# Decoder of four layers: the last cross-attention's maxima, with two steps over the short last piece of keys joined into one

## Chip, core and metric

The kernel runs on one core of a Trainium2 chip. The metric is the device time of one execution in microseconds (us), the median of several runs. Engine names are those of the profile: PE is TensorE's matmul (PEld its weight loads), DVE VectorE, ACT ScalarE, POOL GpSimd, SP SyncE.

## The reference, cut to what matters

The reference is a decoder of four layers, each an attention, a cross-attention with a context of 6404 rows, and a feed-forward part. The change touches the last layer's cross-attention alone. With x of 1024 rows, width 128, 16 heads of 8, the reference does

```
q = split_heads(x @ Wq.T + bq)            # 16 x 1024 x 8
k = split_heads(ctx @ Wk.T + bk)          # 16 x 6404 x 8
v = split_heads(ctx @ Wv.T + bv)
scores = q @ k.T / sqrt(8)                # masked keys: -1e9
ctx = softmax(scores) @ v
out = ctx @ Wo.T + bo
```

For the softmax, each row's largest score is taken off before the exponential. The kernel works out these maxima first ("maxima"), and the scores, exponentials and products with the values after that ("core").

## The kernel before

**Tiles and stages.** Heads go in four groups g of four, and queries in two halves h of 512. A pair of group and half is called a unit here, n = 2g + h, n = 0 to 7. `l3_xattn` (L1783) first has a part that makes keys, queries and values and the maxima of unit 0 with nothing beside them (its `m2` tiles, which hold the maxima's scores in PSUM, have three buffers, L1798). Then a loop over n = 0 to 6 (L1826) runs `pairs_core` for unit n with the maxima of unit n + 1 as its `beside`; here `m2` has two buffers, `s` three and `acc` one (L1819). Unit 7 runs in a stage of its own with nothing beside it.

**Core.** `pairs_core` (L1327) goes over the keys in tiles of 128. 6404 keys make 51 tiles, and the last holds 4 keys. For each tile, and each of two pairs of heads, it makes the scores `s` (keys by 512 queries, one matmul for each of the pair's two heads), and ScalarE takes the exponential into `p` (L1375). Products with the values go into `acc` one tile later (`late`, L1346). After the last tile the values of tiles 49 and 50 follow, then `acc` is copied to `oT` (`copy`, L267: in turn by VectorE, L271, and ScalarE, L273), and `pairs_norm` (L1391) transposes `oT` into an `m2` tile (L1396), takes reciprocals of the sums (L1399) and writes `o` (L1401).

**Maxima.** `pairs_max` (L1281) is a generator. It goes over the keys in pieces of 512, `c` = 0 to 12, of which the last has 260 keys, and over four blocks of 128 queries: 52 steps. A step is called for pair 0 and pair 1; each call takes an `m2` tile, makes two matmuls into it (one for each head) and a reduction by VectorE (L1303) over its 2 x 512 or 2 x 260 elements. After the last step the generator runs `pairs_neg` (L1308): a last reduction `r` (L1313), six casts and two subtractions that split the negated maximum into three parts in `mpad` (L1316 to L1319), and for each pair four transposes of `mpad` into one `m2` tile (L1323) and an addition onto the queries `qP` (L1325). The next unit's scores need these.

**The order around the change.** Scores, maxima and values of these units are held in the order in which they are written (L265). At the head of each tile, `pairs_core` takes a step by `next(beside, None)` (L1354), and calls it for both pairs between the scores of pair 0 and those of pair 1. What the generator has left after the last tile is run behind the last values (L1386). There are 52 steps and 51 tiles, so one step and `pairs_neg` come there. The prologue, the part ahead of unit 0, calls each step by itself. `l0_attn` uses `pairs_max` too, with `causal` set.

Of the kernel before, what the change touches and what calls it, by code (L numbers as in the profile page):

```python
# [25 lines left out]
BANK = 512  # L26
# [185 lines left out]
class Decoder:  # L212
# [1068 lines left out]
    def pairs_max(self, ps, pool, qP, kP, h, mpad, nk=NK, causal=None):  # L1281

        nc = self.nc
        chunks = h + 1 if causal is not None else (nk + BANK - 1) // BANK
        mx = pool.tile([P, 4, 4, chunks], F32, tag="mx", name="mx")
        for c in range(chunks):
            for t in range(4):  # L1290
                q0 = h * BANK + t * P
                a, b = c * BANK, min((c + 1) * BANK, nk if causal is None else q0 + P)

                def step(pair, a=a, b=b, q0=q0, t=t, c=c):
                    diag = causal is not None and b == q0 + P
                    m = ps.tile([P, 2, BANK], F32, tag="m2", name="m2")
                    for j in range(2):
                        r = slice(64 * j, 64 * j + 64)
                        self.matmul(m[:, j, :b - a], lhsT=qP[pair][r, q0:q0 + P], rhs=kP[pair][r, a:b], start=True, stop=not diag)
                    if diag:  # L1300
                        for j in range(2):
                            self.matmul(m[:, j, b - a - P:b - a], lhsT=causal[:, 1, :], rhs=causal[:, 0, :], start=False, stop=True)
                    nc.vector.tensor_reduce(mx[:, t, 2 * pair:2 * pair + 2, c:c + 1], m[:, :, :b - a], AX.X, ALU.max)  # L1303

                yield step
        self.pairs_neg(ps, pool, qP, h, mpad, mx)

    def pairs_neg(self, ps, pool, qP, h, mpad, mx):  # L1308
# [625 lines left out]
```

## Time and profile before

| | us |
|---|---|
| median of 3 runs | 6131.01 (6130.72 to 6139.10) |
| the profiled execution | 6133.59 |
| its span | 6131.8 |
| PE busy | 5705.8 (93%) |
| DVE busy | 3756.3 (61%) |
| ACT busy | 3097.7 (51%) |
| POOL busy | 2254.4 (37%) |
| prologue's maxima, about | 4820 to 4941 |
| units 0 to 6, about | 4941 to 5843 |
| unit 7, about | 5843 to 5940 |

Times inside the span are counted from its start. A line of a timeline gives the start, the length, the engine, the line of the kernel, the operation with the tiles written and read, and how many instructions were merged; in brackets stands how long the engine had been idle and what released it. In a table of stretches the granted clock is TensorE's: 1.00 is full speed. Line numbers are those of the kernel before; those behind L1303 move by 9 or less in the changed one (L1323 becomes L1332).

### The profile page before, as it was taken

How to read it: one execution, taken by the hardware profiler on the slowest of the kernel's cores; microseconds unless marked ns; L12 is line 12 of the kernel's file. 1: busy time of each engine (PE TensorE's matmuls, PEld its weight loads, DVE VectorE, ACT ScalarE, POOL GpSimd, SP SyncE). 2: the span in 40 equal slices, each digit the busy share in tenths (PEclk: the TensorE clock that was granted, in tenths of full speed). 3: DMA queues.
4: the chain of work that ended last, by engine and by line, in shares of the span. 5: the costliest groups of instructions: out<-in, count | busy, mean ns of one | idle time of the engine just before them, and what ended most of it. 6: DMA issues, size and time to landing. Idle time of an engine off the chain costs nothing. (4 is left out here: it accounts for less than half of the span.)

```text
span 6131.8 us, 72192 instructions
## 1 busy us (share of the span) xinstructions
PE 5705.8 (93%) x29144; PEld 2049.1 (33%) x29144; DVE 3756.3 (61%) x4571; ACT 3097.7 (51%) x4041; POOL 2254.4 (37%) x1088
## 2 busy tenths in 40 slices
PE   5899999999999999999899968999989689999999
PEld 2333333333333433333375433111124211111126
DVE  6587777777777777776235461100025799999923
ACT  2434444444444444444321326899941167888872
POOL 2057767676776767678341530100001000000000
PEclk7899999999999999999999978999989689999989
DMA  3000000000000000000000013200022100000000
GB/s 114 4 1 1 1 1 1 1 1 1 1 1 1 1 1 1 1 17 18 30 9 11 1 66 92 77 17 1 1 93 71 54 1 22 1 22 1 1 6 30
DMA packets 65199, 117.97 MB, mean 19 GB/s; under 512 B 10474, under 2 KB 46672, under 8 KB 63200
## 3 DMA queue, kind: packets, MB, share of 16 engines
q1 hardware_dynamic: 64288, 110.08, 5.6%
q8 instruction: 228, 3.74, 0.2%
q10 hardware_dynamic: 576, 3.28, 0.1%
q14 instruction: 107, 0.88, 0.0%
HBM read 81.88 MB, written 31.42 MB: 18 GB/s over the span
## 5 line engine op out<-in xcount | busy, mean ns | idle before, releaser
L741 POOL TENSOR_TENSOR tot<-tot,p 128x1024 f32<-128x1024 f32 (+1 forms) x800 | 1889.6, 2362 | 584.7 <-ACT p L732 569.2
L732 ACT ACTIVATE p<-p,drop,keep 128x1024 f32<-128x1024 f32 (+1 forms) x816 | 1011.8, 1240 | 1321.8 <-DVE p L731 1260.1
L669 DVE TENSOR_REDUCE mx<-m 128x2 f32<-128x1024 f32 (+1 forms) x832 | 982.1, 1184 | 496.5 <-PE m L668 480.0
L1303 DVE TENSOR_REDUCE mx<-m 128x2 f32<-128x1024 f32 (+4 forms) x928 | 1027.0, 1156 | 92.8 <-PE m L265 82.4
L731 DVE TENSOR_TENSOR p<-s,every 128x1024 f32<-128x1024 f32 (+1 forms) x816 | 991.2, 1215 | 73.2 <-PE s L726 34.6
L1375 ACT ACTIVATE p<-s 128x512 f32<-128x512 f32 (+4 forms) x1620 | 819.5, 589 | 239.1 <-PE s L265 238.3
L668 PE MATMUL m<-kT,qT 64*128 64x512 f32 (+1 forms) x3328 | 888.6, 606 | 12.3 <-DVE mx L669 11.6
L1372 ACT ACTIVATE p<-s 128x1024 f32<-128x1024 f32 x918 | 843.9, 1187 | 31.6 <-PE s L1367 24.1
L726 PE MATMUL s<-qT,kT 64*128 64x512 f32 (+1 forms) x3264 | 837.6, 596 | 16.6 <-DVE p L731 15.4
L713 PE MATMUL acc<-p,v 128*64 128x512 f32 (+1 forms) x3264 | 809.4, 606 | 4.8 <-ACT p L732 4.1
L1346 PE MATMUL acc<-p,v 128*8 128x512 f32 (+2 forms) x3672 | 621.9, 597 | 0.0
L265 PE MATMUL m<-kP,qP 64*128 64x512 bf16 (+4 forms) x1856 | 371.5, 396 | 101.8 <-DVE mx L1303 56.9
L726 PEld LDWEIGHTS s<-qT,kT 64*128 64x128 f32 (+1 forms) x3264 | 321.7, 185 | 412.5 <-issue 342.1
L668 PEld LDWEIGHTS m<-kT,qT 64*128 64x128 f32 x3328 | 280.7, 185 | 504.1 <-DVE mx L669 371.6
L265 PE MATMUL acc<-p,v 128*9 128x512 f32 (+2 forms) x3240 | 422.2, 594 | 0.0
L265 PE MATMUL s<-qP,kP 64*128 64x512 bf16 (+4 forms) x1620 | 384.0, 387 | 8.9 <-ACT p L1375 6.1
L713 PEld LDWEIGHTS acc<-p,v 128*64 128x64 f32 (+1 forms) x3264 | 198.8, 136 | 550.8 <-issue 456.1
L1367 PE MATMUL s<-qP,kP 48*128 48x512 bf16 (+2 forms) x1836 | 281.0, 384 | 2.7 <-ACT p L1372 1.9
L271 DVE COPY oT<-acc 128x512 f32<-128x512 f32 x14 | 9.7, 689 | 404.5 <-PE acc L1346 395.7
L387 POOL MEMSET mpad<- 128x512 f32 x2 | 1.1, 530 | 637.0 <-PE m L1456 600.4
L265 PEld LDWEIGHTS <-qP 64*128 64x128 bf16 x1856 | 122.8, 96 | 318.8 <-issue 261.9
L265 PEld LDWEIGHTS <-kP 64*128 64x128 bf16 (+1 forms) x1620 | 83.6, 94 | 352.4 <-issue 347.5
(484 smaller groups left out, 4446.7 us busy)
## 6 DMA issues: line engine op xcount, KB each, us to landing
kd<-part SPq DMA_DIRECT2D x156, 128.0 KB, 1.8
wb<-expert_weights SPq DMA_DIRECT2D x30, 512.0 KB, 3.6
kP<-kd SPq DMA_DIRECT2D x24, 512.0 KB, 3.6
kP<-kd SPq DMA_DIRECT2D x48, 192.0 KB, 4.5
w_expert<-in_Y_w SPq DMA_DIRECT2D x8, 768.0 KB, 4.2
qd<-part SPq DMA_DIRECT2D x36, 128.0 KB, 1.8
qP<-qd SPq DMA_DIRECT2D x16, 256.0 KB, 5.3
ctxT<-in_ctxT ACTq DMA_DIRECT2D x4, 800.5 KB, 6.3
```

Source lines behind the costliest of these rows:

```text
L265: return self.tc.keep_in_program_order(self.nc.tensor.matmul(*a, **k))
L668: nc.tensor.matmul(m[:, j, :b - a], lhsT=qT[r, q0:q0 + P], rhs=kT[r, a:b], start=True, stop=True)
L669: tc.keep_in_program_order(nc.vector.tensor_reduce(mx[:, t, :, c:c + 1], m[:, :, :b - a], AX.X, ALU.max))
L713: nc.tensor.matmul(acc[64 * j:64 * j + 64, :], lhsT=v[:n, t, 64 * j:64 * j + 64], rhs=pr[:n, j, :], start=t == 0, stop=t == NKT - 1, tile_ ...
L726: nc.tensor.matmul(s[:n, j, :], lhsT=kT[r, t * P:t * P + n], rhs=qT[r, hs], start=True, stop=True)
L731: tc.keep_in_program_order(nc.vector.tensor_tensor(pr[:n], s[:n], every[:n], ALU.add))
L732: nc.scalar.activation(pr[:n], pr[:n], AF.Exp, bias=drop[:n, t:t + 1], scale=keep[:n, t:t + 1])
L741: nc.gpsimd.tensor_tensor(tot[:n], tot[:n], pr[:n], ALU.add)
L1303: nc.vector.tensor_reduce(mx[:, t, 2 * pair:2 * pair + 2, c:c + 1], m[:, :, :b - a], AX.X, ALU.max)
L1346: matmul(acc[32 * j:32 * j + v.shape[3], off:], lhsT=v[:n, t, 4 * g + j, :], rhs=ws[j][:n, :BANK - off], start=t == 0, stop=t == nkt - 1, ...
L1372: nc.scalar.activation(p2[:n], both[:n], func)
L1375: nc.scalar.activation(pp[j][:n, :w], ss[j][:n, :w], func)
```

## The change

Steps whose piece has at most 320 keys (BANK * 5 // 8) are not given out at once when `causal` is not set: two are kept and given out as one function that calls both. With 6404 keys these are the four steps of the last piece, so the generator gives 48 + 2 = 50 steps. A joined step calls pair 0 of both steps, then pair 1 of both. The 51st call of `next` then finds no step, and runs what stands behind the loop, `pairs_neg`.

```
+        short = []
         for c in range(chunks):
             for t in range(4):
...
-                yield step
+                if causal is None and b - a <= BANK * 5 // 8:
+
+                    short.append(step)
+                    if len(short) == 2:
+                        one, other = short
+                        short = []
+                        yield lambda pair, one=one, other=other: (one(pair), other(pair))
+                else:
+                    yield step
         self.pairs_neg(ps, pool, qP, h, mpad, mx)
```

## The prediction

> **What bounds the kernel now.** Seen whole, TensorE is busy 93% of the span and VectorE 61%, but that says little about this stage, so I went from the page to the timelines of the last cross-attention. A *unit* is one group of heads by one half of the queries (51 tiles); beside units n = 0 to 6 the maxima of unit n+1 are worked out. On the page, the maxima's reductions are one of the costliest groups:
>
> ```profile
> L1303 DVE TENSOR_REDUCE mx<-m 128x2 f32<-128x1024 f32 (+4 forms) x928 | 1027.0, 1156 | 92.8 <-PE m L265 82.4
> ```
>
> Inside a unit VectorE is the bound: 98 reductions over full pieces run back to back in 114.03 us (timeline of VectorE, from 5200.98), 1.164 us each, so 2.33 us a tile of two; a tile lasts 2.35. What can be won or lost lies at the ends of units. Busy time by stretch, first a unit's inside, then an end (columns: length, busy us and count of TensorE, its weight loads, VectorE, ScalarE, GpSimd, then granted clock and DMA):
>
> ```profile
> 5072.00:5184.00 112.00, 106.57 (x760) 20.75 (x755) 112.00 (x97) 98.53 (x192) 0.00 (x0) 1.00 0.07 21
> 5184.00:5201.00 17.00, 12.52 (x86) 4.26 (x80) 10.71 (x25) 7.14 (x15) 0.00 (x0) 0.81 0.19 65
> ```
>
> TensorE's timeline over the end of unit 0 (start, length, line, tile, count, wait):
>
> ```profile
> 5056.53 0.39 PE L265 MATMUL s<-qP,kP 64*128 64x512 bf16 x2
> 5056.76 0.28 PE L265 MATMUL m<-kP,qP 64*128 64x260 bf16 x2
> 5057.24 0.29 PE L265 MATMUL m<-kP,qP 64*128 64x260 bf16 x2 [0.20 <-DVE mx L1303]
> ...
> 5061.24 0.38 PE L265 MATMUL s<-qP,kP 64*4 64x512 bf16 x2
> ...
> 5062.59 2.15 PE L265 MATMUL acc<-p,v 128*9 128x512 f32 x16
> 5064.67 0.40 PE L265 MATMUL m<-kP,qP 64*128 64x260 bf16 x4
> 5068.68 1.09 PE L1323 MATMUL m<-ident,mpad 128*128 128x128 f32 x4 [3.61 <-DVE mpad L1317]
> 5069.55 1.06 PE L1396 MATMUL m<-ident,oT 128*128 128x128 f32 x4
> 5070.54 1.11 PE L1323 MATMUL m<-ident,mpad 128*128 128x128 f32 x4
> 5071.59 0.43 PE L265 MATMUL s<-qP,kP 64*128 64x512 bf16 x2
> ```
>
> Tile 48 starts at 5056.53, tile 49 at 5058.89, tile 50 (4 keys) at 5061.24. The left-over 52nd step is at 5064.67. Then TensorE waits 3.61 us for the chain of pairs_neg, and the next unit starts at 5071.59. While TensorE waits, the copy of `acc` (0.58 us on ScalarE, from 5064.77) is hidden.
>
> **The change, part by part.** Both programs' orders, compared engine by engine, differ on TensorE and VectorE alone, and only at the ends of units and of the part ahead of them. No instruction goes or comes: VectorE still does eight reductions of 520 elements a unit.
>
> *The doubled steps.* Tiles 48 and 49 now each hold four score pairs and four reductions between `s` of pair 0 and `s` of pair 1, and `m2` has two buffers. The third `m` waits for the first reduction, the fourth for the second, and TensorE, which issues these in order, holds `s` of pair 1 and the values behind them. From the timelines: a reduction of 520 elements starts 0.33 us after its matmul (5061.55 to 5061.88), lasts 0.69, and the next follows after 0.62; its buffer's matmul comes 0.09 after its end. Tile 48 (a run of two full and two short reductions stands in the trace from 5054.83 to 5058.40): the first short one runs 5057.09 to 5057.78, the second ends at 5058.40, the fourth `m` goes at 5058.49, `s` of pair 1 at 5058.60, the values 0.21 later take 0.97 (5060.26 to 5061.24), so tile 49 starts at 5059.78: **+0.89**. Tile 49 in the same way: products at 5060.00, first reduction at 5060.33, fourth product at 5061.73, values done at 5063.02, against 5061.24: **+0.89** again. VectorE does not hide this: 4 x 0.62 = 2.5 us would fit a tile, the ring of two does not.
>
> *The chain moved ahead of tile 50.* The 51st `next()` runs pairs_neg, and its eight transposes stand before tile 50's scores. The last reduction ends at 5062.88. From the part ahead of the units, where nothing else is between, VectorE's and TensorE's rows give the rest:
>
> ```profile
> 4935.14 0.37 DVE L1313 TENSOR_REDUCE r<-mx 128x16 f32<-128x208 f32 x1
> ...
> 4938.19 0.69 DVE L1325 TENSOR_TENSOR qP<-qP,m 128x512 bf16<-128x512 bf16 x1 [1.27 <-PE m L1323]
> ```
>
> ```profile
> 4937.07 1.09 PE L1323 MATMUL m<-ident,mpad 128*128 128x128 f32 x4 [3.33 <-DVE mpad L1317]
> 4938.94 1.11 PE L1323 MATMUL m<-ident,mpad 128*128 128x128 f32 x4 [0.78 <-DVE qP L1325]
> ```
>
> First transposes 1.93 after the chain's start, second ones 3.80 after (they wait for the addition onto qP), TensorE free 1.05 later: 4.85. With the start at 5062.92, tile 50 begins at 5067.77, not 5061.24. TensorE stands idle 1.8 us for `mpad` and 0.8 us for qP; queued behind are all of tile 50's scores, the values of 49 and 50, `oT`'s transposes and the next unit.
>
> *Tile 50 and the end.* From its start to the copy of `acc` the trace has 3.53 us (5061.24 to 5064.77), which four exponentials (2.02) and 16 value products (2.15) set, not the 260-wide products that leave it: 5071.30. Now the copy, 0.58, is bare, then some 0.14 to the transposes and 1.04 for them: next unit at 5073.05, against 5071.59: +1.46. Where VectorE copies (units 1, 3, 5; 0.69) the same steps give 5201.08 against 5199.90: +1.18. One thing is given back: reductions start 1.08 us after the unit's start in most units (5199.90 to 5200.98), 0.71 after unit 0; now qP is long done and only pairs_norm is ahead, about 0.66. So +1.41 for unit 0, +1.04 for 2 and 4, +0.76 for 1, 3 and 5. After unit 6 the next stage waits for all readers; its scores came at 5842.52, now the chain to `o` (copy, 0.14, 1.10 and 0.6 to the end of L1401) ends about 5844.2: +1.66. **Sum: 1.41 + 2.08 + 2.28 + 1.66 = +7.4 us.**
>
> *The clock.* At every end of a unit the granted clock falls to half. In unit 3 TensorE went idle at 5450.0:
>
> ```profile
> 5449.00:5450.00 1.00, 1.00 (x12) 1.00 0.01 2
> 5450.00:5451.00 1.00, 0.01 (x2) 0.80 0.00 0
> 5451.00:5452.00 1.00, 0.00 (x0) 0.50 0.00 0
> ```
>
> It fell 0.6 us into the idle time here and 3.2 us in unit 0; it is half for 3.4, 6.8 or 10.2 us. Now it falls on waits, transposes and copies. After the change the idle time comes some 2 us sooner and ahead of tile 50, so half clock will lie over tile 50's scores and values. What it costs, from the stage that follows unit 6 (first half, then full clock):
>
> ```profile
> 5844.84 2.04 PE L1346 MATMUL acc<-p,v 128*9 128x512 f32 x8
> ...
> 5847.35 1.04 PE L1346 MATMUL acc<-p,v 128*9 128x512 f32 x8
> ```
>
> Sixteen products can cost 2.0 us more and the scores 0.3: 0 to 2.3 a unit. With half clock for one to two spells of 3.4 us from the first fall, some 3 us lie on tile 50 and cost about 1.3. Against it, transposes that now run at 421 ns each may run at 272 (the shortest of L1323): a set of four takes some 0.45 less, two sets at most: 0 to -0.9; I take -0.4. Net +0.9 by seven units: **+6.3 us** (from -6.3 to +16.1).
>
> [...]
>
> *The part ahead of the units.* Its steps are paired too, but the same 104 reductions stand in one queue with three buffers (VectorE busy 116.5 of 121 us), and the 13 steps of the values still fit 50 calls: nothing. l0_attn passes `causal` and is unchanged. DMA issues do not move.
>
> **Sum.** 7.4 + 6.3 = +13.7 us. Against the profiled execution, 6133.6 (span 6131.8), that is 6147.3; the median of the runs shown is 2.6 lower: **6144.7**, slower by 0.22%. Some 0.2%, 12.3 us, is what a measurement of this kernel tells from no change.
>
> **Rivals.** *Same:* the gate opens as soon as transposes run, or it falls late; tile 50 is at full clock. For it: unit 0's half clock lasted 3.4 us only. Then +7.4 alone: **6138.4**. *Clearly slower:* half clock lasts through tile 50 each time: +16.1 + 7.4, and the new start of the units is slow again (0.42 by 5): **6156.6**. [...] *Faster:* the doubled step fits its tile after all, as its VectorE time (2.5 of 2.35 us) nearly does and as VectorE idles 1.03 us in each short tile now; it decides if TensorE does not wait for the ring. Then 1.78 a unit goes: 7.4 - 12.5 = -5.1, and with a clock that stays full up to -6.3 more: **6119.6 to 6125.9**. Against it: with three buffers the part ahead of the units already shows TensorE waiting 0.20 us on each short product.
>
> **How the numbers follow.** Forecast (6139 to 6150) 0.47; same 0.25; clearly slower 0.18; faster 0.10. The bound of 0.2% is 6143.3: some 0.7 of the forecast's chance lies above it, so slower 0.33 + 0.18 = 0.51; faster by over 12.3 us needs the whole of that rival and more, 0.04; the rest, 0.45, is within. The range 6134 to 6158 takes in the forecast, most of "same" and most of "clearly slower", and leaves out some 0.2.
>
> **What would show it.** In the new profile: tiles 48 and 49 at about 3.25 us each, with TensorE waiting for `mx` inside them; L1332's first matmul waiting some 1.8 us for `mpad`, then tile 50's `s` after L1332 and not before; the copy of `acc` with TensorE idle beside it; from tile 48's start to the next unit's some 16.5 us against 15.06; half clock over the 16 value products. It is wrong if tiles 48 and 49 stay near 2.35 us, if the transposes don't hold tile 50, or if the clock stays at 1.00 there.

## The result, and the profile after

| | before | after |
|---|---|---|
| median, us (9 runs each) | 6131.01 (6123.58 to 6139.10) | 6154.23 (6145.69 to 6162.58) |
| the profiled execution | 6133.59 | 6146.94 |
| its span | 6131.8 | 6145.1 |

After by before is 1.0039, with a 95% interval of 1.003 to 1.0047: the change makes the kernel slower; the medians lie 23.2 us apart. The forecast was 6144.7; the time lies in the range, near the case called "clearly slower" (6156.6). The profiled execution is the second shortest of the nine, and that of before lies 2.6 us above its median, so the two traces show 13.3 us of the loss and not all of it.

VectorE's work is what it was. On the page of the changed kernel, the maxima's reductions have the same number, and a mean of 1157 ns where it was 1156:

```profile
L1304 DVE TENSOR_REDUCE mx<-m 128x2 f32<-128x1024 f32 (+4 forms) x928 | 1025.8, 1157 | 83.6 <-PE m L265 73.1
```

The stretch of units 0 to 6, first before, then after (length, busy us and count of TensorE, its weight loads, VectorE, ScalarE, GpSimd, granted clock, DMA share, GB/s):

```profile
4949.00:5843.00 894.00, 827.78 (x5802) 173.49 (x5798) 849.55 (x825) 735.30 (x1424) 0.00 (x0) 0.98 0.03 8
```

```profile
4945.00:5857.00 912.00, 838.70 (x5802) 169.06 (x5800) 849.63 (x825) 737.54 (x1424) 0.00 (x0) 0.96 0.03 8
```

The stretch is 18 us longer, with the same 5802 matmuls, the same VectorE time, and 10.9 us more of TensorE's busy time: the same instructions took longer, at a clock of 0.96 in place of 0.98. The rest is idle time.

TensorE's waits in this stretch show what the change traded. Before, then after (engine and line, what it waited for: total, times, longest):

```profile
PE m L1323 <- DVE mpad L1317: 26.0, 7, 4.0
PE m L265 <- DVE mx L1303: 3.5, 14, 0.4
```

```profile
PE m L265 <- DVE mx L1304: 14.6, 41, 0.7
PE m L1332 <- DVE mpad L1326: 11.6, 7, 1.7
PE m L1332 <- DVE qP L1334: 5.5, 7, 0.8
...
PE m L1405 <- ACT oT L273: 2.9, 4, 0.8
PE m L1405 <- DVE oT L271: 2.6, 3, 0.9
```

The wait for `mpad` fell from 26.0 to 11.6 us; the wait for the ring of `m2` (its two buffers, taken in turn) rose from 3.5 to 14.6, one of 5.5 for qP is new, and so is one of 5.5 for the copy of `acc`, which stood hidden before. With some small ones all of TensorE's waits went from 33.3 to 41.6 us.

TensorE's timeline over the end of unit 1 (tile 48 starts at 5186.10):

```profile
5190.73 0.29 PE L265 MATMUL m<-kP,qP 64*128 64x260 bf16 x2 [0.69 <-DVE mx L1304]
5191.33 0.29 PE L265 MATMUL m<-kP,qP 64*128 64x260 bf16 x2 [0.32 <-DVE mx L1304]
...
5191.77 1.04 PE L265 MATMUL acc<-p,v 128*9 128x512 f32 x8
5194.46 1.09 PE L1332 MATMUL m<-ident,mpad 128*128 128x128 f32 x4 [1.65 <-DVE mpad L1326]
5196.33 1.11 PE L1332 MATMUL m<-ident,mpad 128*128 128x128 f32 x4 [0.78 <-DVE qP L1334]
...
5199.14 3.72 PE L265 MATMUL acc<-p,v 128*9 128x512 f32 x16
5203.75 1.11 PE L1405 MATMUL m<-ident,oT 128*128 128x128 f32 x4 [0.89 <-DVE oT L271]
5204.80 0.61 PE L265 MATMUL s<-qP,kP 64*128 64x512 bf16 x2
```

Each wait of the prediction is here: the third and fourth `m` of tile 49 wait 0.69 and 0.32 us, the first transposes 1.65 us for `mpad`, the second 0.78 us for qP, and only then does tile 50 start. But from 5194.46 on the products also last longer: eight value products took 1.04 us just before, and sixteen take 3.72, where the next view has 2.15. The same program, same engine, at the end of unit 4:

```profile
5590.08 0.63 PE L1332 MATMUL m<-ident,mpad 128*128 128x128 f32 x4 [1.65 <-DVE mpad L1326]
5591.49 0.66 PE L1332 MATMUL m<-ident,mpad 128*128 128x128 f32 x4 [0.78 <-DVE qP L1334]
...
5593.43 2.15 PE L265 MATMUL acc<-p,v 128*9 128x512 f32 x16
5596.26 0.66 PE L1405 MATMUL m<-ident,oT 128*128 128x128 f32 x4 [0.68 <-ACT oT L273]
5596.84 0.39 PE L265 MATMUL s<-qP,kP 64*128 64x512 bf16 x2
```

The two waits are the same to a hundredth, but transposes take 0.63 and 0.66 instead of 1.09 and 1.11, and the sixteen products 2.15. The end of a unit, from tile 48's start to the next unit's first `s`, takes 18.69 us in unit 1 and 15.13 in unit 4. Before the change these took 15.44 and 15.07, with half clock on their transposes. So a changed end at full clock is as long as the end before; one at half clock is 2.4 to 3.5 us longer.

All seven ends, in us (the column "values" goes from tile 50's start to the copy of `acc`: 3.54 at full clock, up to 5.63 at half):

| unit | end before | end after | values after |
|---|---|---|---|
| 0 | 15.06 | 18.53 | 5.63 |
| 1 | 15.44 | 18.69 | 5.63 |
| 2 | 15.07 | 17.46 | 5.42 |
| 3 | 15.43 | 15.24 | 3.54 |
| 4 | 15.07 | 15.13 | 3.54 |
| 5 | 15.43 | 17.78 | 5.63 |
| 6 | 15.51 | 15.87 | 3.54 |
| sum | 106.99 | 118.69 | |

The ends give +11.7 us. The next units' first tiles give 6.1 more: from a unit's start to its tile 48 before took 112.9 to 113.3 us; after, 114.7 to 114.8 in units 1 to 4, 112.82 in unit 5, which starts at full clock, and 113.25 in unit 6. That makes 17.8. What lies ahead of unit 0 was 3.8 us shorter in this execution, and what follows unit 7's start, which the change does not touch, 0.7. Ahead of unit 0 steps are joined too, but a difference of 3.8 us there is not told from chance: experiments 4 and 6 below have the same program up to unit 0, and their traces differ by 8.3 us there. 17.8 - 3.8 - 0.7 = 13.3, the difference of the two profiled executions.

### The profile page after: what moved, and what is told of

Its sections match the earlier page's. It is cut to its first block, busy times and chain, and to the rows that moved or that the text cites. A ratio compares the mean times of both kernels' runs of the same rounds, so it can differ in the third digit from the quotient of the medians.

```text
span 6145.1 us, 72188 instructions
## 1 busy us (share of the span) xinstructions
PE 5713.0 (93%) x29144; PEld 2041.8 (33%) x29144; DVE 3755.8 (61%) x4571; ACT 3099.8 (50%) x4041; POOL 2254.1 (37%) x1088
## 5 line engine op out<-in xcount | busy, mean ns | idle before, releaser
L1304 DVE TENSOR_REDUCE mx<-m 128x2 f32<-128x1024 f32 (+4 forms) x928 | 1025.8, 1157 | 83.6 <-PE m L265 73.1
L668 PE MATMUL m<-kT,qT 64*128 64x512 f32 (+1 forms) x3328 | 889.9, 607 | 11.5 <-DVE mx L669 11.1
L265 PE MATMUL m<-kP,qP 64*128 64x512 bf16 (+4 forms) x1856 | 376.0, 399 | 112.7 <-DVE mx L1304 68.5
L265 PE MATMUL acc<-p,v 128*9 128x512 f32 (+2 forms) x3240 | 430.8, 605 | 0.0
L265 PE MATMUL s<-qP,kP 64*128 64x512 bf16 (+4 forms) x1620 | 382.8, 391 | 9.3 <-ACT p L1384 6.7
L265 PEld LDWEIGHTS <-qP 64*128 64x128 bf16 x1856 | 123.7, 96 | 328.2 <-issue 269.4
L265 PEld LDWEIGHTS <-kP 64*128 64x128 bf16 (+1 forms) x1620 | 83.6, 94 | 349.7 <-issue 345.2
```

Source lines behind the costliest of these rows:

```text
L265: return self.tc.keep_in_program_order(self.nc.tensor.matmul(*a, **k))
L668: nc.tensor.matmul(m[:, j, :b - a], lhsT=qT[r, q0:q0 + P], rhs=kT[r, a:b], start=True, stop=True)
```

## The experiments

Two theories of the loss. **Clock:** the idle time ahead of tile 50 makes the clock fall to half, and it stays there over the values and into the next unit. **Place and ring:** the waits themselves cost the time, those for the ring of two in tiles 48 and 49 or those of TensorE, whose instructions are held in the order in which they are written (L265), behind the chain; half clock only comes along. Short diffs are against the changed kernel unless another is named. Ratios are to the kernel before, run beside each.

**1. The chain behind the values again.** An empty 51st step lets the generator reach pairs_neg behind the last values, as before. The joined steps stay.

```
+        if causal is None:
+            yield lambda pair: None
         self.pairs_neg(ps, pool, qP, h, mpad, mx)
```

> The joined steps stay, but a 51st, empty step puts pairs_neg behind the last values again. Theory: what costs time in the change is that the chain stands ahead of tile 50 (TensorE idle there, and half clock over tile 50's work and the next unit's first tiles). Then: tiles 48 and 49 still 3.33 us each, tile 50 to the copy 3.54 in every unit, the chain done beside tile 50, first transposes without a wait; from tile 48 to the next unit about 13.1 us against 15.07 and 15.43 before, so 2.0 to 2.4 us a unit less, 14 to 19 us in all: ratio to before about 0.997. Rival 'the ring': the joined steps themselves, held by two buffers, are the cost. Then it stays slower than before, by 7 x 1.96 = 14 us or more: ratio 1.002 to 1.004.

Measured: 6116.21 against 6134.70, ratio 0.997 (0.9959 to 0.9982). TensorE's timeline at the end of unit 1:

```profile
5189.02 2.15 PE L265 MATMUL acc<-p,v 128*9 128x512 f32 x16
5191.10 0.66 PE L1334 MATMUL m<-ident,mpad 128*128 128x128 f32 x4
...
5193.14 0.39 PE L265 MATMUL s<-qP,kP 64*128 64x512 bf16 x2
```

No wait is left at `mpad`: the chain runs on VectorE while TensorE does tile 50. Tiles 48 and 49 take 3.33 and 3.32 us, so the ring's hold is all there, and still an end takes 12.11 us instead of 15.06 (12.94 in unit 6). The ring as the cause of the loss falls. The joined steps alone make the kernel faster: the last reductions come in tile 49, no step is left over, and the chain has tile 50 to run beside. The change loses by where it puts the chain. The starts take 6 us of the ends' 21.4 back in this execution: in units 2, 4 and 6 the clock falls some 3.8 us in, for 3.41 us, and tile 48 comes after 114.9 us.

**2. One joined step only.** Two of the four short steps are joined, so that 51 steps stand beside 51 tiles, and the chain comes behind the values.

```
-                if causal is None and b - a <= BANK * 5 // 8:
+                if causal is None and b - a <= BANK * 5 // 8 and t < 2:
```

> Only two of the four short steps are joined, so 51 steps stand beside 51 tiles and pairs_neg falls behind the last values. Theory: one hold (0.98 us) instead of two; the last reductions lie beside tile 50, mpad is ready about 3.9 us after tile 50's start, some 0.4 us after the values' end; from tile 48 to the next unit about 12.5 us, 2.6 to 2.9 a unit less than before, 18 to 20 us in all: ratio 0.997, a little below the kernel with both pairs joined and the chain behind. Rival 'the ring': one hold costs a half of the change's loss, ratio about 1.002.

Measured: 6109.05, ratio 0.996 (0.9946 to 0.9973). The profiled execution is the slowest of the five (6117.98). Tile 48 takes 3.33 us and tile 49 2.35; the ends sum up to 87.9 us, against 85.6 in experiment 1, and the two ratios' intervals overlap: which of the two is better isn't told by this. Half the hold in place of the whole shortens the ends of units 0 and 4 (11.70 and 11.69), but those of units 1, 3 and 5, where VectorE copies `acc`, take 12.92 to 13.73: the first transposes come 10.81 us after tile 48's start there, and 9.60 elsewhere. Experiments 4 and 6 show why, in an order with the same lag.

**3. The idle time filled.** The changed kernel, with seven matmuls ahead of the transposes that read old queries and write into the tile that the transposes then overwrite: useless work of 1.69 us. The order and the place of the chain are those of the changed kernel.

```
+        o = (1 - h) * BANK
+        for k in range(idle):      # idle = 7
+            self.matmul(m[:, k % 2, :], lhsT=qP[0][:, o:o + P], rhs=qP[1][:, o:o + BANK], start=True, stop=True)
```

> The changed kernel with seven matmuls of 512 columns added ahead of the transposes of pairs_neg, into the tile that these overwrite: some 1.5 us of work in the 1.65 us in which TensorE waits for mpad. Theory 'clock': the cost of the change is half clock over tile 50 and the next unit's start (tile 50 to the copy took 5.63 us at half clock and 3.54 at full clock in the profile after). If the work keeps the clock full, every unit's end is like that of unit 4, 15.1 us, and the time comes back to that of before: ratio 0.999 to 1.001. Rival 'place': the waits alone cost, whatever the clock; then nothing changes, ratio 1.003 to 1.005. If 0.8 us of waiting for qP is enough to halve the clock, the ratio lies between.

Measured: 6139.84, ratio 1.0005 (0.9996 to 1.0014). TensorE's timeline at the end of unit 1:

```profile
5188.23 1.69 PE L265 MATMUL m<-qP 128*128 128x512 bf16 x7
5189.86 0.66 PE L1335 MATMUL m<-ident,mpad 128*128 128x128 f32 x4
...
5193.23 2.15 PE L265 MATMUL acc<-p,v 128*9 128x512 f32 x16
```

The transposes start about when they did (1.56 us after tile 49's values, 1.65 without the added work), and tile 50 stands behind them as in the changed kernel. But tile 50 takes 3.54 us to its copy in all seven units, and the ends sum up to 106.97 us, against 118.69 without the added work and 106.99 before the change. With the idle time filled and nothing moved, the loss is gone, to within the interval. The theory of the clock stands; that the place alone would keep the kernel slower, by 1.003 to 1.005, falls. Half clock is not gone altogether: it still came four times. At 5451.37 it came just as the copy of `acc` began; the other three times, as at 5584.49 and 5714.20, the copy's idle time (0.7 to 0.8 us) lay in the 3.41 us before the fall. In three units the first tiles took some 2 us more.

**4. The eight calls dealt out by 3, 3, 2.** The four short steps have two calls each. Instead of four to each of two tiles, three go to tile 48, three to 49 and two to 50: two at their usual places and the third behind the scores of pair 1. The chain comes behind the values.

```
+                    short += [(step, 0), (step, 1)]
+                    if t == 3:
+                        for i in (0, 3, 6):
+                            yield lambda k, some=short[i:i + 3]: [one(pair) for one, pair in some[k:k + 1]]
...
+                elif step:
+                    step(2)
```

> The kernel before with the eight calls of the four short steps dealt out 3, 3 and 2 to tiles 48, 49 and 50, the third call behind the scores of pair 1, so that no score waits for the ring; pairs_neg behind the last values. Theory: tiles 48 and 49 stay within 0.2 us of 2.35, the left-over step is gone, from tile 48 to the next unit about 11.6 us, 3.5 to 3.8 a unit less than before, 24 to 27 us in all: ratio 0.996. Rival 'the ring' expects a gain as well; a rival 'hidden anyway' (the left-over step lay beside the chain's wait) expects 0.999 to 1.000.

Measured: 6109.72, ratio 0.9958 (0.9946 to 0.9971). Tiles 48 and 49 take 2.51 and 2.49 us, so the ring's hold is nearly gone, and ends take 11.01 in units 0 and 2. In units 1, 3 and 5 they take 12.59 to 13.05. VectorE's timeline in unit 1:

```profile
5190.81 0.69 DVE L271 COPY oT<-acc 128x512 f32<-128x512 f32 x1 [0.20 <-PE acc L265]
...
5191.69 0.48 DVE L1342 MEMSET acc<- 128x512 f32 x1
5192.08 0.17 DVE L1324 CAST mpad<-part 128x16 f32<-128x16 bf16 x1
```

The copy of `acc` stands in VectorE's queue among the casts and subtractions of the chain, waits 0.20 us for the last value product and takes 0.69; a memset of 0.48 stands ahead of the last cast. The transposes of `mpad` wait for that last cast, and come at 10.13 us instead of 8.91 after tile 48's start.

**5. The kernel before, its idle time filled.** The kernel before has idle time too, 3.2 to 4.0 us a unit. Fifteen useless matmuls as in experiment 3 were put there.

> The kernel before with fifteen matmuls of 512 columns ahead of the transposes of pairs_neg, some 3.2 us of work in the 3.6 to 4.0 us in which TensorE waits for mpad, into the tile that these overwrite. Theory 'clock': the wait halves the clock in the kernel before too, there over transposes (421 ns instead of 272) and the first tiles of the next unit. With the clock kept full, a set of four transposes takes some 0.45 us less, twice a unit, and the reductions start 0.35 us sooner: about 1 us a unit, 6 to 9 us in all, ratio 0.9985 to 0.999. Rival 'place': the clock does not matter, ratio 1.000. If the clock falls nevertheless, the added work takes 6.4 us instead of 3.2 and the kernel is slower by up to 20 us.

Measured: 6128.88 against 6132.79, ratio 0.9992 (0.9983 to 1.0001). In units 0, 2 and 4 the clock stays full and ends take 14.42 to 14.43 us, some 0.64 less than before. The added work puts the first transposes off by 0.31 us there (12.45 after tile 48's start, against 12.14), so that the transposes at half clock had cost some 0.9 us. But in units 1 and 3 the clock fell about when the added work began, which took 5.08 us in unit 1 and held the end up: 16.49 and 16.39.

```profile
5193.26 5.08 PE L265 MATMUL m<-qP 128*128 128x512 bf16 x15 [1.06 <-DVE mx L1303]
```

The sum of ends, 106.2, is hardly below 107.0. At most a small gain, and none that the interval shows.

**6. As 4, with `acc` always copied by ScalarE.** This takes the copy out of the chain's way on VectorE.

```
-        self.copy(oT, acc)
+        if wide or causal is not None:
+            self.copy(oT, acc)
+        else:
+            nc.scalar.copy(oT, acc)
```

> The kernel with the short steps' calls dealt out 3, 3 and 2, and the copy of acc in units 0 to 6 always by ScalarE. In the profile of the dealt-out kernel the units whose copy VectorE makes end 1.2 us later (first transposes 10.13 us after tile 48's start, against 8.91), because the copy stands ahead of the rest of the chain in VectorE's queue and waits there for the last values. Theory: then all units end about 11.0 us after tile 48's start, 1.6 to 2.0 us less in three units, 5 to 6 us in all: ratio to before 0.9945 to 0.995. Rival: the difference is the clock's spells and not the queue; then ratio 0.996, as without it.

Measured: 6099.87 against 6132.79, ratio 0.9954 (0.994 to 0.9967), the lowest of all. Ends take 11.01, 11.15, 11.02, 11.01, 11.31, 11.80 and 12.20 us, 79.5 in all, against 84.4 in experiment 4. TensorE's timeline at the end of unit 1:

```profile
5179.01 0.38 PE L265 MATMUL s<-qP,kP 64*4 64x512 bf16 x2
...
5180.36 2.15 PE L265 MATMUL acc<-p,v 128*9 128x512 f32 x16
5182.93 0.63 PE L1330 MATMUL m<-ident,mpad 128*128 128x128 f32 x4 [0.41 <-DVE mpad L1324]
```

Tile 50 (from 5179.01) follows tile 49 with no wait, and of the chain 0.41 us is left to wait for. The first transposes come 8.91 or 8.92 us after tile 48's start in all seven units, so the queue on VectorE was the cause of their lag in units 1, 3 and 5. That 6 beats 4 as a whole rests on the ends; the two ratios' intervals overlap, and of the 11.9 us between the two profiled executions 8.3 lie ahead of unit 0. Because `copy` alternates, the seven copies left out of it also swap the engines of the copies behind unit 6; from unit 7's start the program took 290.2 us here, and 288.5 in experiment 4.

**7. How little work is enough.** The changed kernel as in experiment 3, with three matmuls instead of seven in the wait of 1.65 us.

```
+        for k in range(idle):      # idle = 3
```

> The changed kernel with three matmuls ahead of the transposes instead of seven: 0.65 us of work, 1.0 us of idle time left. Theory 'clock': with less work in the wait the clock falls more often than with seven and less often than with none: ratio between 1.0005 (seven) and 1.0039 (none). Rival 'place': 1.003 to 1.005. If a threshold of idle time decides, it falls together with one of the two ends.

Measured: 6133.33 against 6132.79, ratio 1.0000 (0.9991 to 1.0009). The three take 0.82 us, not the 0.65 that was expected, and half the wait is left, as TensorE's timeline in unit 1 shows:

```profile
5184.27 0.82 PE L265 MATMUL m<-qP 128*128 128x512 bf16 x3
5185.89 0.66 PE L1335 MATMUL m<-ident,mpad 128*128 128x128 f32 x4 [0.80 <-DVE mpad L1326]
```

The profiled execution (6126.85) is the third shortest of eleven. Ends take 15.06 to 15.17 us in units 0 to 4; unit 5 alone had half clock over its values (17.64), and unit 6 took 15.81. Three do as well as seven, within the intervals. So the loss does not follow the idle time in proportion.

## Why the prediction was right, and which sizes were wrong

**The doubled steps: right.** Tile 48 was worked out at 3.25 us and takes 3.33; the hold of the ring in tile 49 is there too. Experiment 1 shows what the sum did not say by itself: this hold, nearly 2 us a unit, is more than paid for by the left-over step that goes. (The prediction says that VectorE's 4 x 0.62 = 2.5 us would fit a tile of 2.35; it would not quite, but the ring's hold of 0.98 us is the longer one.)

**The chain ahead of tile 50: right.** First transposes were worked out at 8.32 us after tile 48's start, and come at 8.36. The waits of 1.65 and 0.78 us were called 1.8 and 0.8.

**Half clock over tile 50: right in four units of seven, and it decides.** Tile 50 to the copy takes 5.63 us in three units and 5.42 in one, where 3.53 plus at most 2.3 was given; in units 3, 4 and 6 it takes 3.54, as before.

**The split of the sum: wrong.** The +7.4 us for the new order was worked out with rows of transposes at half clock (1.09 and 1.11 us for four), because this part of the trace of before has no others (417 ns is its shortest there), and the credit for full clock, -0.4 by seven units, stood in the other term. At full clock transposes take 0.63 to 0.66, and each of the three sets on the path gives back some 0.45 us. The order then adds nothing to what the kernel before took: 15.13 against 15.07 in unit 4, and ratios of 1.0005 and 1.0000 in experiments 3 and 7. No unit's end took the 16.5 us that the prediction named as a sign: three took 15.1 to 15.9, four 17.5 to 18.7. With full clock on both sides, experiments 3 and 7 have ends of 15.06 and 15.17 (copy by ScalarE and by VectorE), and experiment 5 has 14.43 and 14.80, of which some 0.3 is the delay by the added work. By these an estimate of what the new order costs by itself is 0.7 to 0.9 us a unit, 5 to 6 in all; the kernel before lost as much by its transposes at half clock.

**The +6.3 us for the clock: too small.** It counted 3 us of half clock over tile 50 and full clock after that. Three stretches of the changed kernel of 3.41 us each, around the fall in unit 1 (columns as above):

```profile
5190.99:5194.40 3.41, 1.50 (x14) 0.23 (x11) 3.08 (x12) 1.09 (x2) 0.00 (x0) 1.00 0.00 0
5194.40:5197.81 3.41, 2.57 (x11) 1.52 (x12) 1.02 (x2) 0.00 (x0) 0.00 (x0) 0.50 0.00 0
5197.81:5201.23 3.42, 3.17 (x16) 0.25 (x16) 0.36 (x1) 2.02 (x4) 0.00 (x0) 0.50 0.16 39
```

In units 0 and 1 the spell of half clock lasted 17.07 us, in units 2 and 5 13.65 and 10.24, where before it had been 3.4 to 10.2. So it covers the transposes, all sixteen products, the copy and often the next unit's first tiles, which take 1.5 to 1.9 us more in four units (in unit 4 by a fall of its own, 0.4 us into the unit). The prediction had the new start in its rival (0.42 by 5) and not in its sum. The four slow ends give 3.47 + 3.25 + 2.39 + 2.35 = 11.5 us, the starts of units 1 to 6 some 6.0: together 17.5 of the 17.8 us that this stretch lost. So in the two traces the clock took 17.5 us where 6.3 was given, and the order, as what is left, 0.3 where 7.4 was given. That the sum, +13.7, is so near the 13.3 between the two profiled executions is luck: the two errors, and 4.5 us by which this execution was shorter outside the stretch, cancel. The medians lie 23.2 apart. "Clearly slower" is near in its total (6156.6 against 6154.23) and not in its parts: it took half clock over tile 50 for all seven units and kept the 7.4. What "same" rested on, tile 50 at full clock, held in three units of seven.

The nine runs' times go with the mean granted clock: 0.951 at 6145.69, 0.950 at 6146.94, 0.948 at 6150.91 and 6156.12, 0.946 at 6162.58. That the runs longer than the profiled one had more ends at half clock is inferred from this; only one execution has a trace.

**The length of the waits.** In the kernel before, the clock fell 0.6 us into a wait of 3.98 us (unit 3). In the changed kernel the waits ahead of tile 50 last 1.65 and 0.78 us, and half clock still lay over tile 50 in four units of seven; filling the first wait took the loss away (experiment 3: ratio 1.0005 against 1.0039).

**Where the change's gain went.** An end goes from 15.06 to 12.11 us with the steps joined and the chain behind the values (experiment 1), and back to 15.1 with the chain ahead of tile 50 (unit 4; experiment 3). Half clock then adds 2.4 to 3.5 us to an end where it comes, and in four units the first tiles take 1.5 to 1.9 more.

## What to carry to other kernels

Put instructions that wait for a long chain of another engine behind work of their own engine that is ready (experiment 1 against the change: ratios of 0.997 and 1.0039). A generator that runs out of steps one call early moves its tail, too, and that tail should be looked at by itself. Before counting a short wait as so many microseconds, look at the granted clock behind it: in the changed kernel the same wait of 1.65 us stood in an end that was as long as before (unit 4: 15.13 us, 15.07 before) and in one that was over 3 us longer (unit 1: 18.69, 15.44 before). And a copy that alternates between engines has a place in each engine's queue; where a chain runs in one of them, the other was the better place here (experiment 6: ends of 79.5 us in all, 84.4 in experiment 4).

## What the runs showed of the hardware that was not expected

In the trace of the changed kernel the clock falls and rises on a grid of 3.413 us: three of its falls, at 5061.28, 5194.40 and 5330.93, lie 133.12 and 136.53 us apart, 39 and 40 times 3.413, and the spells of half clock behind units 0 to 6 are 3.41, 6.83, 10.24, 13.65 or 17.07 us long, one to five times 3.413.

In these traces TensorE's busy time does not tell by itself whether the clock falls. In the stretch ahead of the fall in unit 1 TensorE was busy for 1.50 of 3.41 us (above); in this one of unit 4 for 1.49, and the clock stayed full behind it:

```profile
5586.62:5590.03 3.41, 1.49 (x13) 0.23 (x11) 3.07 (x12) 1.09 (x2) 0.00 (x0) 1.00 0.00 0
```

And at half clock TensorE was busy for 3.17 of 3.42 us (5197.81 to 5201.23) and the clock did not rise. In experiment 3 the clock fell behind a stretch in which TensorE was busy for 2.82 us, and a stretch that was busy throughout at half clock was followed by another at half clock, up to 5591.32:

```profile
5447.96:5451.37 3.41, 2.82 (x20) 0.32 (x16) 0.67 (x2) 2.02 (x4) 0.00 (x0) 1.00 0.19 39
...
5584.49:5587.90 3.41, 3.41 (x14) 0.49 (x16) 3.26 (x4) 2.83 (x7) 0.00 (x0) 0.50 0.03 7
```

What decides stays open. Useless work of 0.82 us in a wait of 1.65 us left one fall over the values in place of four, and gave the changed kernel its 0.4% back.
